# Cross-attention's mask and normalisation bias in the last row of the keys, in a transformer stack on one core

## The chip, the cores and the metric

The kernel runs on one core of a Trainium2 chip. The metric is the device time of one execution in microseconds (us). The core has TensorE (PE, matmuls; its weight loads are shown as PEld), VectorE (DVE), ScalarE (ACT), GpSimd (POOL) and SyncE (SP, which here issues the DMAs). Each engine works through its own instructions in the order in which they stand in the program, and waits for others by semaphores.

## What is computed

The reference is a stack of four blocks on x of 8 x 256 x 128, with a context of 8 x 64 x 64: a gated cross-attention (L0), a small cross-attention (L1), six decoder layers (L2) and a last attention with a softmax over the queries (L3). All is in float32. The change touches the second attention of each decoder layer. Cut to it:

```python
def _ln(x, g, b, eps=1e-05):
    m = jnp.mean(x, axis=-1, keepdims=True)
    v = jnp.mean(jnp.square(x - m), axis=-1, keepdims=True)
    return (x - m) / jnp.sqrt(v + eps) * g + b

def _mha(s, t, kv_w, q_w, o_w, o_b, mask):          # 16 heads of 64
    k, v = jnp.split(s @ kv_w, 2, axis=-1)
    q = t @ q_w
    ...
    scores = jnp.einsum('bhqd,bhkd->bhqk', q, k) * D ** (-0.5)
    scores = jnp.where(mask[:, None] == 0, jnp.float32(-1000000000.0), scores)
    attn = jax.nn.softmax(scores, axis=-1)
    o = jnp.einsum('bhqk,bhkd->bhqd', attn, v)
    ...
    return o @ o_w + o_b

def step(t, p):                                     # six times
    tn = _ln(t, norm_g, norm_b)
    t = _mha(tn, tn, skv, sq, sow, sob, tgt_mask) + t
    tn = _ln(t, norm_g, norm_b)
    t = _mha(src, tn, ckv, cq, cow, cob, src_mask) + t
    tn = _ln(t, pg, pb)
    t = t + (jax.nn.relu(tn @ w1 + b1) @ w2 + b2)
```

src is the context (64 keys for each batch entry), src_mask says which keys are hidden. norm_g and norm_b are one pair of vectors for all layers.

## The kernel before

The residual t stays in SBUF, two tiles of 128 rows for each of the 8 batch entries b.

**Order of the work.** Every stage registers small functions with at(tick, phase, function). At the end they are called in order of tick, then phase, and each engine's instructions are chained in just this order. So a tick is a round of the software pipeline, and the phase says where in the round a step stands in the queues of PE, DVE, ACT and POOL. In a layer, self-attention takes 4 ticks for each b (32 ticks), cross-attention 2 (16 ticks), the feed-forward 1 (8 ticks). T_ca is the first tick of a layer's cross-attention; b has its ticks T = T_ca + 2b and T + 1. Steps reach into the stages before and after.

**Folded weights.** Cross-attention's query and key weights are multiplied into one matrix AT for each head, and its value and output weights into WVO (plan_ca_weights). This is done at the end of self-attention: AT in tick T_ca - 4, WVO in T_ca - 3 (PE L1042, copies L1054 and L1052 on ACT). Then the keys of a head are AT times the context: they stand in the 128 dimensions of the normalised row, so that no query projection is left. keys_both makes the keys of two batch entries at once, in phase 3.7 of the ticks T_ca - 2, T_ca + 2, T_ca + 6, T_ca + 10: 16 matmuls into each of two PSUM tiles (L1079; the profile counts each float32 matmul of this form as two), and four copies to SBUF by ACT (L1085).

**Normalised rows.** ahead does them: statistics on DVE (L808, L809, phase 6 of tick T - 4, in the same tick as the keys for every second b), the scales on POOL (L814 to L821, phase 8.4), x minus mean times rstd on ACT (L827), a transpose on PE (L841), and, on the way out of PSUM, a multiplication by norm_g and an addition of norm_b on ACT (L843).

**A unit.** plan_weights_64 does a unit, 128 rows (one qt of a b), with 16 heads of 64 keys in a PSUM tile of two banks:

- scores, phase 1 of its tick: 16 matmuls in float32 (L341) and, after each four of them, four mask matmuls in bf16 (L348). A mask matmul has a stationary operand of zeros with ones in row 0, and a moving one, nm2, with 0 or -1e30 in row 0, so that it adds the mask to each row.
- lower, phase 2: ACT copies the scores to SBUF (e, L357), DVE takes each head's maximum (m, L359), POOL subtracts it (L360)
- exps, phase 8: exp on ACT (L366)
- divide, phase 2.4 of the next tick: sum and reciprocal on DVE (L370, L371), multiplication on POOL (L372)
- turn, phase 2.5 of the tick after: 32x32 transposes on DVE (L380)
- sums, phase 3.0 of the third tick after: 16 matmuls with the values (L388), and DVE adds the result to the residual (L1104)

The residual's bias is added by POOL (L290, phase 7), and the values are made by L303 (PE) and L309 (ACT).

**Self-attention beside it.** A tick there holds two units: scores L898, mask and minimum in one DVE operation (L912), exp on ACT (L917), the reciprocal L925 on DVE, the division L927 on POOL, transposes L937 on DVE, values L953 on PE with evictions L284 (DVE) and L286 (ACT), output projection L971 and its addition L978 on DVE (phase 8.2 of its tick).

**Buffers.** PSUM is a pool of four tiles of two banks, which all matmul results share. The SBUF tag "o" has four buffers, for self-attention's outputs, the folding and the feed-forward.

Of the kernel before, what the change touches and what calls it, by code (L numbers as in the profile page):

```python
# [8 lines left out]
F32 = mybir.dt.float32  # L9
I32 = mybir.dt.int32  # L10
BF16 = mybir.dt.bfloat16
AF = mybir.ActivationFunctionType
ALU = mybir.AluOpType
AX = mybir.AxisListType
PSUM = bass.MemoryType.PSUM

P = 128
B, S, D = 8, 256, 128
M, DM = 64, 64
NL, H, HD, FF = 6, 16, 64, 512  # L20
HC = H * HD // P
NT = B * S // P
QT = S // P
BIG = 1.0e30
# [3 lines left out]
def tile_xattn_stack(ctx: ExitStack, tc: tile.TileContext, io, out: bass.AP):  # L28
    nc = tc.nc

    const = ctx.enter_context(tc.tile_pool(name="const", bufs=1))
# [25 lines left out]
    def big(tag, bufs=4, shape=(P, 1024), dtype=F32):  # L57

        return heap.tile(list(shape), dtype, tag=tag, name=uniq(tag), bufs=bufs)
# [4 lines left out]
    def sm(shape, tag):  # L64
        return small.tile(shape, F32, tag=tag, name=uniq(tag))

    def load_const(name, shape):
        t_ = const.tile(shape, F32, tag=name, name=name)
        nc.sync.dma_start(out=t_, in_=io[name])
        return t_  # L70
# [7 lines left out]
    def column(name):  # L78
        v = io[name]
        t_ = const.tile([v.shape[0], 1], F32, tag=name, name=name)  # L80
        nc.sync.dma_start(out=t_, in_=v.unsqueeze(1))
        return t_
# [70 lines left out]

    norm_g = column("L2_norm_g")
    norm_b = column("L2_norm_b")
    pre_g = load_const("L2_pre_gT", [D, NL])
    pre_b = load_const("L2_pre_bT", [D, NL])
    ff_b1 = load_const("L2_ff_b1T", [P, NL, FF // P])
# [88 lines left out]
        return nm  # L247


    nm2 = const.tile([P, B, M], BF16, tag="nm2", name="nm2")  # L250
    nc.vector.memset(nm2, 0.0)
    ones0 = const.tile([P, 32], BF16, tag="ones0", name="ones0")
    nc.vector.memset(ones0, 0.0)
    nc.vector.memset(ones0[0:1], 1.0)


    def stats(xin, eps):
# [21 lines left out]
    def at(tick, phase, fn):  # L279
        plan.setdefault(tick, []).append((phase, fn))  # L280
# [30 lines left out]
        )  # L311
        return vw

    def plan_weights_64(tick, qt, qT, keys, values, mask, take):

        tl = {}

        def scores():  # L320
            sc = two_banks("sc").rearrange("p (q x) -> p q x", q=4)
            if mask is None:
                for i in range(4):
                    for a in range(4):
                        q = (i + 2 * (a // 2)) % 4
                        rows = slice(64 * (a // 2), 64 * (a // 2) + 64)
                        qb = 4 * qt + q
                        nc.tensor.matmul(
                            sc[32 * a : 32 * a + 32, q, :],
                            lhsT=qT()[rows, qb * 32 : (qb + 1) * 32],  # L330
                            rhs=keys()[rows, 4 * (a % 2) : 4 * (a % 2) + 4, :].rearrange(
                                "p h k -> p (h k)"
                            ),
                            start=True, stop=True,
                        )
                tl["sc"] = sc.rearrange("p q x -> p (q x)")
                return
            for q in range(4):
                qb = 4 * qt + q
                for a in range(4):  # L340
                    nc.tensor.matmul(  # L341
                        sc[32 * a : 32 * a + 32, q, :],
                        lhsT=qT()[:, qb * 32 : (qb + 1) * 32],
                        rhs=keys()[:, a].rearrange("p h k -> p (h k)"),
                        start=True, stop=False,
                    )
                for a in range(4):
                    nc.tensor.matmul(  # L348
                        sc[32 * a : 32 * a + 32, q, :], lhsT=ones0, rhs=mask,
                        start=False, stop=True,  # L350
                    )
            tl["sc"] = sc.rearrange("p q x -> p (q x)")

        def lower():
            sc = tl.pop("sc")
            e = big("e", shape=(P, 16, M))
            nc.scalar.copy(e.rearrange("p h k -> p (h k)"), sc)  # L357
            m = sm([P, 16], "m16")
            nc.vector.tensor_reduce(m, sc.rearrange("p (h k) -> p h k", k=M), AX.X, ALU.max)  # L359
            nc.gpsimd.tensor_tensor(  # L360
                e, e, m.unsqueeze(2).to_broadcast([P, 16, M]), ALU.subtract
            )
            tl["e"] = e

        def exps():
            nc.scalar.activation(tl["e"], tl["e"], AF.Exp)  # L366

        def divide():
            r = sm([P, 16], "r16")
            nc.vector.tensor_reduce(r, tl["e"], AX.X, ALU.add)  # L370
            nc.vector.reciprocal(r, r)  # L371
            nc.gpsimd.tensor_tensor(  # L372
                tl["e"], tl["e"], r.unsqueeze(2).to_broadcast([P, 16, M]), ALU.mult
            )

        def turn():
            e = tl.pop("e").rearrange("p (q h) (k x) -> p (h k) q x", q=4, x=32)
            eT = big("k", shape=(P, 8, 4, 32))
            for i in range(2):
                nc.vector.transpose(eT[:, 4 * i : 4 * i + 4], e[:, 4 * i : 4 * i + 4])  # L380
            tl["eT"] = eT

        def sums():
            ps = mm_tile()
            eT, vw = tl.pop("eT"), values()
            for s in range(8):
                g, r, k = s // 4, s // 2 % 2, s % 2
                nc.tensor.matmul(  # L388
                    ps[:, :D], lhsT=eT[:, s].rearrange("p q x -> p (q x)"),
                    rhs=vw[:, r, k, g, :], start=(s == 0), stop=(s == 7),  # L390
                )
            take(ps)

        at(tick, 1, scores)
        at(tick, 2, lower)
        at(tick, 8, exps)
        at(tick + 1, 2.4, divide)
        at(tick + 2, 2.5, turn)
        at(tick + 3, 3.0, sums)
# [212 lines left out]

    def mask_keys():
        mi = big("q", dtype=I32)
        mi = mi[0:1, : B * M].rearrange("p (b m) -> p b m", b=B)
        nc.sync.dma_start(out=mi, in_=io["mask_Bx1xS2_if1"].rearrange("b o m -> o b m"))
        nc.vector.tensor_scalar(nm2[0:1], mi, 0.0, -BIG, ALU.is_equal, ALU.mult)

    mask_bf = []

# [41 lines left out]
    def plan_l0(b, T):  # L662
        st = {}
# [67 lines left out]
        at(T + 2, 3.2, make_values)  # L731
        for qt in range(QT):
            plan_weights_64(
                T + qt, qt, lambda: st["q"], lambda: st["k"], lambda: st["VW"], None,
                lambda ps, qt=qt: add(qt, ps),
            )
        at(T + 4, 6, moments)
# [267 lines left out]
    def plan_ca_weights(l, T):  # L1005
# [54 lines left out]
            at(T - 4 + i, -0.5, lambda i=i: fetched(i))  # L1060
        at(T + 1, 8.05, regrouped)
        at(T + 2, 3.6, folded("AT", 0, lambda c: st[1][:, :, c, :], HD ** -0.5))
        at(T + 3, 3.6, folded("WVO", 1, lambda c: W["ca", l][2][:, c, :]))

    keys_of = {}

    def plan_ca(l, b, T):
        st = {}
        fold = W["fold", l]

        def keys_both():

            res = [big("q", shape=(D, 4, 4, M)) for _ in range(2)]
            for g in range(2):
                ps = two_banks("mm").rearrange("p (r a x) -> p r a x", r=2, a=4)
                for a in range(4):
                    for r in range(2):
                        rows = slice(r * DM, (r + 1) * DM)
                        nc.tensor.matmul(  # L1079
                            ps[:, r, a, :], lhsT=fold["AT"][rows, 4 * g + a, :],  # L1080
                            rhs=ctx2[rows, b : b + 2, :].rearrange("p b m -> p (b m)"),
                            start=True, stop=True,
                        )
                for i in range(2):
                    nc.scalar.copy(  # L1085
                        res[i][:, :, 2 * g : 2 * g + 2, :].rearrange("p a r k -> p r a k"),
                        ps[:, :, :, i * M : (i + 1) * M],
                    )
            keys_of[b], keys_of[b + 1] = res

        def make_values():
            st["VW"] = values_of(b, fold["WVO"])

        def res():
            st["tb"] = residual(b, W["ca", l][3])

        ahead(b, (T - 4, 6), (T - 3, 2.95), (T - 2, 2.9), norm_g, norm_b, st)
        if b % 2 == 0:
            at(T - 2, 3.7, keys_both)
        at(T + 2, 3.2, make_values)  # L1100
        at(T + 2, 7, res)

        def add(qt, ps):
            nc.vector.tensor_add(t[:, QT * b + qt, :], ps[:, :D], st["tb"][:, qt, :])  # L1104

        for qt in range(QT):
            plan_weights_64(
                T + qt, qt, lambda: st["tT"], lambda: keys_of[b], lambda: st["VW"],
                nm2[:, b].unsqueeze(1).to_broadcast([P, 4, M]), lambda ps, qt=qt: add(qt, ps),
            )  # L1110

    def plan_ff(l, b, T):
# [136 lines left out]
    last = {}  # L1249
# [68 lines left out]
```

## Time and profile before

| | us |
|---|---|
| median of three runs (2488.26 to 2490.18) | 2489.39 |
| the profiled execution | 2494.55 |
| its span, first to last instruction | 2492.8 |

The granted TensorE clock was 0.981 on average. In the first decoder layer the engines are busy as follows (us):

| stretch (us) | PE | DVE | ACT | POOL |
|---|---|---|---|---|
| 402 to 492, cross-attention of layer 0 (90) | 86.65 | 66.09 | 55.41 | 73.42 |
| 580 to 740, self-attention of layer 1 (160) | 160.00 | 137.12 | 126.14 | 86.09 |

The costliest groups are self-attention's (L917, L927, L912, L937, L953, L898). Of the lines named above, the page's list by groups has for cross-attention's parts (L0 uses the same helper for the unit, so counts of 112 hold 96 of cross-attention):

| line, engine | what | count | mean ns |
|---|---|---|---|
| L341 PE | scores, 128x256 f32 | 3072 | 382 |
| L357 ACT | copy of the scores | 112 | 999 |
| L359 DVE | maximum | 112 | 1224 |
| L360 POOL | subtraction | 112 | 1903 |
| L366 ACT | exp | 112 | 1063 |
| L370 DVE | sum | 112 | 1209 |
| L372 POOL | multiplication | 112 | 1902 |
| L380 DVE | transposes | 224 | 660 |
| L1085 ACT | copy of keys, 128x512 | 96 | 600 |
| L978 DVE | addition, 128x256, PSUM and SBUF | 48 | 388 |

A line of the profile's groups reads: line, engine, operation, tiles written and read, shapes, count, then busy time, mean time of one in ns, and the idle time of the engine before it with what ended it. In a timeline, the first number is the start in us from the span's start, the second the time that the merged instructions took, and a bracket at the end is the engine's idle time before it and who ended it. Matmuls overlap, so that the time of one is not its share of PE.

### The profile page before, as it was taken

How to read it: one execution, taken by the hardware profiler on the slowest of the kernel's cores; microseconds unless marked ns; L12 is line 12 of the kernel's file. 1: busy time of each engine (PE TensorE's matmuls, PEld its weight loads, DVE VectorE, ACT ScalarE, POOL GpSimd, SP SyncE). 2: the span in 40 equal slices, each digit the busy share in tenths (PEclk: the TensorE clock that was granted, in tenths of full speed). 3: DMA queues.
4: the chain of work that ended last, by engine and by line, in shares of the span. 5: the costliest groups of instructions: out<-in, count | busy, mean ns of one | idle time of the engine just before them, and what ended most of it. 6: DMA issues, size and time to landing. Idle time of an engine off the chain costs nothing.

```text
span 2492.8 us, 100152 instructions
## 1 busy us (share of the span) xinstructions
PE 2373.5 (95%) x42411; PEld 1749.2 (70%) x42411; DVE 1832.2 (74%) x5988; ACT 1725.5 (69%) x4528; POOL 1448.8 (58%) x2483
## 2 busy tenths in 40 slices
PE   8999999999999999999989999989999989999996
PEld 4667777676777676777776776776777777777774
DVE  4777887738887738888748888747888756888764
ACT  4577777667777657777657777657778657778651
POOL 3755556835556845556845555854556864555763
PEclk8999999999999999999999999999999999999997
DMA  6000022000022000022000012000012000010000
GB/s 174 2 4 18 20 77 56 2 12 20 20 70 63 2 12 20 20 62 67 6 7 24 20 54 71 11 3 20 20 55 78 12 3 20 20 42 23 2 1 18
DMA packets 102834, 76.89 MB, mean 31 GB/s; under 512 B 8113, under 2 KB 96881, under 8 KB 102386
## 3 DMA queue, kind: packets, MB, share of 16 engines
q1 hardware_dynamic: 101794, 70.16, 10.0%
q8 instruction: 334, 5.47, 0.9%
q14 instruction: 114, 0.93, 0.1%
q10 hardware_dynamic: 592, 0.33, 0.1%
HBM read 62.07 MB, written 8.39 MB: 28 GB/s over the span
## 4 chain that ended last, share of the span: by engine, by line
PE 69%; POOL 13%; DVE 8%; ACT 7%; issue 3%; POOLq 0%; DVEq 0%; ACTq 0%
PE mm L953 14%; PE mm L861 13%; PE sc L898 13%; PE mm L971 7%; PE mm L880 7%; POOL e L360 6%; PE mm L1120 3%; PE mm L1137 3%; DVE m L359 3%; POOL e L372 3%; ACT e L357 2%; PE mm L388 2%; ACT e L917 2%; DVE e L912 1%; PE sc L341 1%
## 5 line engine op out<-in xcount | busy, mean ns | idle before, releaser
L927 POOL TENSOR_SCALAR e<-e,rs 128x256 f32<-128x256 f32 x1536 | 702.5, 478 | 672.8 <-DVE rs L925 664.2
L917 ACT ACTIVATE e<-e,mn 128x256 f32<-128x256 f32 x1536 | 758.3, 495 | 145.7 <-DVE mn L912 141.5
L912 DVE CUSTOM_DVE_ANT_0 e<-sc,nm 128x256 f32<-128x256 f32 x1536 | 542.2, 418 | 98.7 <-PE sc L898 98.5
L937 DVE STREAM_TRANSPOSE eTc<-e 128x512 f32<-128x512 f32 x768 | 519.7, 697 | 69.1 <-POOL e L927 67.3
L953 PE MATMUL mm<-eTc,v 32*64 32x256 f32 x12288 | 377.6, 384 | 14.2 <-DVE eTc L937 7.0
L898 PE MATMUL sc<-k,q 64*32 64x256 f32 x12288 | 379.4, 380 | 6.2 <-DVE mn L912 4.2
L953 PEld LDWEIGHTS mm<-eTc,v 32*64 32x64 f32 x12288 | 283.2, 134 | 105.4 <-issue 25.0
L898 PEld LDWEIGHTS sc<-k,q 64*32 64x32 f32 x12288 | 220.7, 106 | 128.9 <-issue 48.9
L360 POOL TENSOR_TENSOR e<-e,m 128x1024 f32<-128x1024 f32 x112 | 213.1, 1903 | 132.1 <-DVE m L359 132.1
L917 ACT ACTIVATION_READ_ACCUMULATOR e<-e,mn 128x1 f32 x1536 | 287.2, 187 | 0.0
L359 DVE TENSOR_REDUCE m<-sc 128x16 f32<-128x1024 f32 x112 | 137.1, 1224 | 167.2 <-ACT e L357 167.2
L388 PE MATMUL mm<-v,k 128*128 128x128 f32 x1792 | 231.4, 284 | 5.4 <-DVE k L380 4.9
L388 PEld LDWEIGHTS mm<-v,k 128*128 128x128 f32 x1792 | 214.6, 196 | 26.9 <-issue 10.7
L341 PE MATMUL sc<-q,tT 128*32 128x256 f32 x3072 | 217.1, 382 | 0.0
L372 POOL TENSOR_TENSOR e<-e,r 128x1024 f32<-128x1024 f32 x112 | 213.0, 1902 | 0.7 <-DVE r L371 0.7
L366 ACT ACTIVATE e<-e 128x1024 f32<-128x1024 f32 x112 | 119.0, 1063 | 115.8 <-POOL e L360 115.8
L861 PE MATMUL mm<-tT,w_sk 128*128 128x256 f32 x768 | 189.6, 390 | 0.0
L971 PEld LDWEIGHTS mm<-w_sow,o 128*128 128x128 f32 x1536 | 175.1, 192 | 16.7 <-issue 14.4
L880 PE MATMUL mm<-w_sv,tT 128*32 128x256 f32 x3072 | 185.7, 382 | 0.0
L971 PE MATMUL mm<-w_sow,o 128*128 128x128 f32 x1536 | 183.4, 278 | 0.9 <-ACT WVO L1052 0.9
L286 ACT COPY v<-mm 128x1024 f32<-128x1024 f32 x96 | 97.1, 1012 | 120.7 <-PE mm L880 120.1
L861 PE MATMUL mm<-tT,w_sq 128*128 128x256 f32 x768 | 173.6, 379 | 0.0
(209 smaller groups left out, 3506.5 us busy)
## 6 DMA issues: line engine op xcount, KB each, us to landing
nm<-mask_d SPq DMA_DIRECT2D x192, 128.0 KB
wd<-o SPq DMA_DIRECT2D x48, 128.0 KB
w_sk<-in_L_sa_kv_dram SPq DMA_DIRECT2D x6, 512.0 KB
w_sv<-in_L_sa_kv_dram SPq DMA_DIRECT2D x24, 128.0 KB
w_sq<-in_L_sa_q_dram SPq DMA_DIRECT2D x6, 512.0 KB
w_sow<-in_L_sa_ow_dram SPq DMA_DIRECT2D x6, 512.0 KB
w_ckv<-in_L_ca_kv_dram SPq DMA_DIRECT2D x12, 256.0 KB
w_cq<-in_L_ca_q_dram SPq DMA_DIRECT2D x6, 512.0 KB
```

Source lines behind the costliest of these rows:

```text
L360: nc.gpsimd.tensor_tensor(e, e, m.unsqueeze(2).to_broadcast([P, 16, M]), ALU.subtract)
L372: nc.gpsimd.tensor_tensor(tl["e"], tl["e"], r.unsqueeze(2).to_broadcast([P, 16, M]), ALU.mult)
L388: nc.tensor.matmul(ps[:, :D], lhsT=eT[:, s].rearrange("p q x -> p (q x)"), rhs=vw[:, r, k, g, :], start=(s == 0), stop=(s == 7),)
L861: nc.tensor.matmul(ps[:, i * S : (i + 1) * S], lhsT=w[:, c * P : (c + 1) * P], rhs=st["tT"], start=True, stop=True,)
L880: nc.tensor.matmul(ps[32 * a : 32 * a + 32, i, :], lhsT=st["tT"][:, kb * 32 : (kb + 1) * 32], rhs=sv[:, a].rearrange("p g x -> p (g x)"), ...
L898: nc.tensor.matmul(sc[32 * a : 32 * a + 32, r, j, :], lhsT=st["q"][g][rows, a, qb * 32 : (qb + 1) * 32], rhs=st["k"][g][rows, a, :], start ...
L912: nc.vector.tensor_tensor_reduce(e[:, i, :], sc4[:, i, :], st["nm"][:, 2 * jj + i % 2, :], -1.0, 3.0 * BIG, ALU.add, ALU.min, mn[:, i : i ...
L917: nc.scalar.activation(e[:, i, :], e[:, i, :], AF.Exp, scale=-1.0, bias=mn[:, i : i + 1], accum_out=rs[:, i : i + 1],)
L927: nc.gpsimd.tensor_scalar(e[:, i, :], e[:, i, :], rs[:, i : i + 1], 1.0, ALU.mult, ALU.mult)
L937: nc.vector.transpose(eT[:, r, :, 2 * jj : 2 * jj + 2, :], e[:, 2 * r : 2 * r + 2, :].rearrange("p j (k x) -> p k j x", x=32),)
L953: nc.tensor.matmul(ops[a // 2][r * HD : (r + 1) * HD, a % 2, :S], lhsT=st["v"][kb // 4][rows, kb % 4, (2 * g + r) * HD : (2 * g + r + 1) * ...
L971: nc.tensor.matmul(st["ps"][:, j * D : (j + 1) * D], lhsT=st["oT"][c // 4][:, c % 4, j * P : (j + 1) * P], rhs=sow[:, c, :], start=(c == 0 ...
```

## The change

Rows of a normalised x have mean zero, so the sum over the 128 dimensions of x times a constant is zero: a number may be subtracted from all the entries of a key without a change of its scores. The changed kernel takes the last entry of the key from all of them (weigh, on the rows of AT, which it first multiplies by norm_g). The last dimension is then free. The row gets a constant 1 there (ahead is given last_off as scale and last_on as bias: 1 and 0 for all dimensions, 0 and 1 for the last), and the key gets there the sum of AT times norm_b, and the mask. The mask is added as the keys leave PSUM, from nm2, which now has 128 rows in float32 and is 0 but for its last row. The mask matmuls go, and with them their operand ones0. The copies of the keys by ACT become additions by DVE.

weigh stands in phase 2.9 of tick T_ca - 3 (T is T_ca - 6 in plan_ca_weights), between the fold of AT and that of WVO.

```diff
@@ tile_xattn_stack, constants
+    norm_rows = const.tile([P, 2, D], F32, tag="norm_rows", name="norm_rows")
+    for i, name in enumerate(("L2_norm_g", "L2_norm_b")):
+        nc.sync.dma_start(out=norm_rows[:, i, :], in_=io[name].partition_broadcast(P))
...
-    nm2 = const.tile([P, B, M], BF16, tag="nm2", name="nm2")
-    nc.vector.memset(nm2, 0.0)
-    ones0 = const.tile([P, 32], BF16, tag="ones0", name="ones0")
-    nc.vector.memset(ones0, 0.0)
-    nc.vector.memset(ones0[0:1], 1.0)
+    nm2 = const.tile([P, B, M], F32, tag="nm2", name="nm2")
+    last_on = ident[:, P - 1 : P]
+    last_off = const.tile([P, 1], F32, tag="last_off", name="last_off")
+    nc.vector.tensor_scalar(last_off, last_on, -1.0, 1.0, ALU.mult, ALU.add)
+    last_big = const.tile([P, 1], F32, tag="last_big", name="last_big")
+    nc.vector.tensor_scalar(last_big, last_on, -BIG, None, ALU.mult)
@@ plan_weights_64, scores
                         rhs=keys()[:, a].rearrange("p h k -> p (h k)"),
-                        start=True, stop=False,
-                    )
-                for a in range(4):
-                    nc.tensor.matmul(
-                        sc[32 * a : 32 * a + 32, q, :], lhsT=ones0, rhs=mask,
-                        start=False, stop=True,
+                        start=True, stop=True,
                     )
@@ mask_keys
-        mi = mi[0:1, : B * M].rearrange("p (b m) -> p b m", b=B)
-        nc.sync.dma_start(out=mi, in_=io["mask_Bx1xS2_if1"].rearrange("b o m -> o b m"))
-        nc.vector.tensor_scalar(nm2[0:1], mi, 0.0, -BIG, ALU.is_equal, ALU.mult)
+        mi = mi[:, : B * M].rearrange("p (b m) -> p b m", b=B)
+        nc.sync.dma_start(
+            out=mi, in_=io["mask_Bx1xS2_if1"].rearrange("b o m -> (b o) m").partition_broadcast(P)
+        )
+        nc.vector.tensor_scalar(nm2, mi, 0.0, last_big, ALU.is_equal, ALU.mult)
@@ plan_ca_weights
+        def weigh():
+
+            AT = st["AT"]
+            g, bias = (
+                norm_rows[:, i].unsqueeze(1).to_broadcast([P, HC, D]) for i in range(2)
+            )
+            z = big("o", shape=(P, HC, D))
+            nc.gpsimd.tensor_tensor(z, AT, bias, ALU.mult)
+            add = sm([P, HC], "add")
+            nc.vector.tensor_reduce(add, z, AX.X, ALU.add)
+            nc.gpsimd.tensor_tensor(AT, AT, g, ALU.mult)
+            last = sm([P, HC], "last")
+            nc.gpsimd.tensor_copy(last, AT[:, :, D - 1])
+            nc.gpsimd.tensor_tensor(
+                AT, AT, last.unsqueeze(2).to_broadcast([P, HC, D]), ALU.subtract
+            )
+            nc.gpsimd.tensor_copy(AT[:, :, D - 1], add)
+
+        at(T + 3, 2.9, weigh)
@@ plan_ca, keys_both
                 for i in range(2):
-                    nc.scalar.copy(
-                        res[i][:, :, 2 * g : 2 * g + 2, :].rearrange("p a r k -> p r a k"),
-                        ps[:, :, :, i * M : (i + 1) * M],
-                    )
+                    for r in range(2):
+                        nc.vector.tensor_tensor(
+                            res[i][:, :, 2 * g + r, :], ps[:, r, :, i * M : (i + 1) * M],
+                            nm2[:, b + i].unsqueeze(1).to_broadcast([P, 4, M]), ALU.add,
+                        )
@@ plan_ca
-        ahead(b, (T - 4, 6), (T - 3, 2.95), (T - 2, 2.9), norm_g, norm_b, st)
+        ahead(b, (T - 4, 6), (T - 3, 2.95), (T - 2, 2.9), last_off, last_on, st)
```

More of the change, by code (lines that the diff above doesn't have):

```diff
@@ L312, in values_of, with plan_weights_64 @@
         return vw
-    def plan_weights_64(tick, qt, qT, keys, values, mask, take):
+    def plan_weights_64(tick, qt, qT, keys, values, halves, take):
         tl = {}
@@ L321, in scores @@
             sc = two_banks("sc").rearrange("p (q x) -> p q x", q=4)
-            if mask is None:
+            if halves:
                 for i in range(4):
@@ L733, in plan_l0 @@
             plan_weights_64(
-                T + qt, qt, lambda: st["q"], lambda: st["k"], lambda: st["VW"], None,
+                T + qt, qt, lambda: st["q"], lambda: st["k"], lambda: st["VW"], True,
                 lambda ps, qt=qt: add(qt, ps),
@@ L1108, in plan_ca @@
                 T + qt, qt, lambda: st["tT"], lambda: keys_of[b], lambda: st["VW"],
-                nm2[:, b].unsqueeze(1).to_broadcast([P, 4, M]), lambda ps, qt=qt: add(qt, ps),
+                False, lambda ps, qt=qt: add(qt, ps),
             )
```

## The prediction

> **What bounds the kernel now.** I read the page first, then the busy time by stretch, the chain of waits inside one cross-attention stage, and last the timelines of DVE, POOL and ACT there. The page says PE:
>
> ```profile
> PE 2373.5 (95%) x42411; PEld 1749.2 (70%) x42411; DVE 1832.2 (74%) x5988; ACT 1725.5 (69%) x4528; POOL 1448.8 (58%) x2483
> PE 69%; POOL 13%; DVE 8%; ACT 7%; issue 3%; POOLq 0%; DVEq 0%; ACTq 0%
> L348 PE MATMUL sc<-nm,ones 128*32 128x256 bf16 x1536 | 112.3, 273 | 0.0
> ```
>
> L348 are the mask matmuls that go. Their 112.3 us is a union with matmuls running beside them, so it is no price. The PE timeline of one unit (a half batch entry, one tick) gives it:
>
> ```profile
> 421.03 0.64 PE L341 MATMUL sc<-q,tT 128*32 128x256 f32 x8
> 421.48 0.29 PE L348 MATMUL sc<-nm,ones 128*32 128x256 bf16 x4
> 421.59 0.61 PE L341 MATMUL sc<-q,tT 128*32 128x256 f32 x8
> ```
>
> From 421.48 to 421.59, four mask matmuls hold PE 0.11 us. There are four such groups in a unit (0.43 us) and 96 units: 41.5 us of PE. Whether that is time gained depends on the stage. The chain of waits in cross-attention (layer 0; start, duration, engine, tile, line):
>
> ```profile
> 442.34 1.90 POOL e L360
> 444.24 1.86 POOL e L372
> 446.10 0.69 POOL tb L290
> 446.79 0.08 issue
> 446.87 0.23 POOL ve L814
> ...
> 448.47 1.87 POOL e L360
> 450.39 0.94 issue
> 451.33 1.00 ACT e L357
> 452.35 1.24 DVE m L359
> 453.66 1.90 POOL e L360
> ```
>
> No PE in it. Two ticks take 11.32 us (442.34 to 453.66). In the first, 6.09 us, POOL has no gap: subtract, multiply, residual, scales, next subtract. The second, 5.23 us, is a loop: subtract 1.90, exp on ACT (the 0.94 "issue"), copy of the next scores 1.00, maximum on DVE 1.24, next subtract. Starts of L360 read from the trace: in all six layers the 15 gaps after the first are 5.23, 5.23, 8.42, 5.23, 6.09, 5.23, 6.09 and so on, alike within 0.01. Only the 8.42 has PE in it: the third unit, where PE still has the last output projection, values and keys to do. The stretch of four ticks (us, then PE, PEld, DVE, ACT, POOL busy):
>
> ```profile
> 441.52:463.90 22.38, 21.95 (x356) 16.13 (x356) 16.97 (x33) 14.34 (x20) 19.04 (x18) 1.00 0.01 2
> ```
>
> PE's 21.95 us fits inside the 22.63 us of two periods: it is nearly full but waits for the loop, so its relief there is not time. Where the new DVE work lands is the question:
>
> ```profile
> 444.75 0.25 DVE L1104 TENSOR_TENSOR t<-mm,tb 128x128 f32<-128x128 f32 x1
> 444.93 0.27 DVE L808 BATCH_NORM_STATS2 six<-t 128x6 f32<-128x128 f32 x1
> ...
> 445.63 0.18 DVE L809 BATCH_NORM_AGGREGATE mv<-six 128x2 f32<-128x6 f32 x1
> 446.96 1.23 DVE L359 TENSOR_REDUCE m<-sc 128x16 f32<-128x1024 f32 x1 [1.16 <-ACT e L357]
> ```
>
> In this tick (keys matmuls at 441.52) phase 3.7 lies between L1104 and L808. POOL's L814 reads mv, ready 445.81, and starts 446.87: 1.06 us of slack.
>
> [...] the copy L357 ends 452.33 and L359, which reads the same scores, starts 452.35. [...] with the scores ready, the copy at 451.33 still waits behind the exp of the unit before. So an add queued ahead of the statistics delays them. [...] in the window 490 to 500 us, with PE idle 2.6 us, the granted clock is 0.83. [...] L978, the same form, shows 0.39.
>
> **The change, part by part.**
>
> *Mask matmuls gone:* minus 0.43 us of PE a unit. In the loop worth nothing; in the third unit's tick two units' worth (0.87) is on PE's path.
>
> *Keys to DVE:* four ACT copies of 0.60 (2.05 us in sequence) become eight adds of 128x256 from PSUM on DVE. L978 starts its follower 0.31 us later, L912 (also PSUM, 256) 0.345; I take 0.32, so 2.6 us; both ends 2.5 and 2.8. In the ticks of pairs 3 and 4 (7th and 11th unit) mv comes at 445.81 + 2.6 = 448.41, L814 starts 0.1 later (as at 408.92 after 408.82), at 448.5 rather than 446.87: +1.64. The subtract behind it moves from 448.47 to 450.1; the maximum (448.5 to 449.7) is in time. The rest of the loop has no slack to take it back: +1.64 each, 3.3 a layer (bounds 1.5 and 1.8 each). ACT's relief brings the exp 0.4 us forward (444.64 to 444.27), off this path. PSUM: the two key tiles are held until about 448.2 instead of 444.8; PE, now 20.2 us of work in 24.3, can bear it.
>
> *weigh, once a layer, at T+3, 2.9* (tick T_ca-3): POOL, behind its first divide (ends 387.67), does three 128x1024 operations (1.90 each, as L372), two small copies (about 0.2 each), then the residual and the second divide: 388.35 becomes 394.4. DVE's reduction (1.21, as L370) is queued behind the reciprocal at 385.60 and ahead of the eviction at 385.66: it waits for z until 389.55 and ends 390.75. Then 0.57 eviction, reciprocal, transposes 1.25: the next scores pass on DVE starts 392.75 instead of 390.00, +2.75.
>
> *Keys of pair 1, tick T_ca-2:* the second transposes wait for POOL's late divide (396.3, end 397.0); then eight adds 2.6, statistics 0.9, transposes 1.3, L978: the scores pass comes at 402.3 instead of 397.82, +4.5. Through the last tick, where DVE had 0.97 us of idle to give back, the first cross maximum moves from 405.60 to 409.45: +3.9 (bounds: 1.5 if PE's waits there absorb more, 5 if the late eviction also holds back PE's PSUM tiles).
>
> *Third unit's tick:* PE restarts with the values at 407.59 + 4.0; the masks give back 0.87. Keys adds follow PE's two key groups, statistics, L978, maximum: subtract at 17.4 us after PE's restart, before 18.2. So 4.0 - 0.8 = about 3.3; rounded up 3.5 for the wait on the second key group. Bound above: PE waited here for L978 (0.17 us, all layers), which now stands behind the adds; if the scores keep that PSUM tile, +2.9 more.
>
> *The rest:* two broadcast loads at the start, a mask load that is wider (read at 153.2 us, issued at 121.7, so 30 us of cover), nm2 in f32, column constants: nothing; without cover, about 1 us once.
>
> Sum a layer: 3.5 + 3.3 = 6.8; six layers 40.8. After cross-attention comes the feed-forward, whose first ticks wait for POOL's scales too (PE idle 2.62 at 493.6), so nothing is taken back. The profiled run, 2494.55 (span 2492.8 and 1.75 around it), would become 2535.4; it stands 5.2 above the median, 2489.39, to which I add the same: **2530 us**.
>
> **Rivals.** (1) PE is what counts, and the adds hide in DVE's idle time (DVE is busy 16.97 of 22.38): the 41.5 us of masks are gained, less perhaps 1 us a layer for weigh: 2454. It decides where PE's own work is longer than the loop: after the change, if two ticks of the loop took less than PE's 10.1 us. For it: PE 95% busy. Against: the chain without PE, and POOL waiting for mv. (2) Only the loop's +3.3 a layer comes, weigh's block being absorbed by the self-attention tail, and the 0.8 is gained: 2.5 x 6 = 15: 2504. For it: DVE idles 1.58 and 0.71 us there. Against: the block is longer than all of it. (3) As forecast, and the scores wait for L978's tile: 9.7 a layer, 58: 2548. With half clock windows after PE's new gaps (1.7 us each), to 2558. (4) Gains and losses cancel: 2489; it needs weigh hidden and the adds under 0.14 us each, since 1.06 us is the slack for eight.
>
> **How the numbers follow.** Forecast (2515 to 2540) 0.50; (3) 0.22; (2) 0.14; (1) and what is faster otherwise 0.10; (4) 0.04. The range 2500 to 2556 leaves out (1), (4) and the top of (3), 0.17. What a measurement can tell from no change is about 0.2%, 5 us. Faster 0.10, same 0.04, slower 0.86.
>
> **What would show it.** In the changed trace: gaps between starts of the L360 subtract after the 7th and 11th unit 7.7 instead of 6.09, the others still 5.23 and 6.09; L814 released by DVE mv there; the eight adds 0.32 us apart just ahead of L808; DVE idle about 4 us before weigh's reduction, released by POOL z; the first cross subtract 4 us later against the last self-attention scores; the granted clock as before. The forecast is wrong if the cross stage gets shorter than 86.1 us (first to last subtract), which would mean PE held it; or if weigh's reduction waits for nothing.

## The result, and the profile after

The changed kernel took 2580.03 us (median of four, 2577.85 to 2583.40), the kernel before beside it 2489.78 us: a ratio of 1.0361, with a 95% interval of 1.0342 to 1.0380. It is slower by 90 us. The forecast had the side right and the size too small: 2530, with a range up to 2556.

The page of the changed kernel, PE and the others, and the shares of the chain that ended last:

```profile
PE 2400.6 (93%) x40875; PEld 1747.5 (68%) x40875; DVE 1900.2 (74%) x6185; ACT 1678.2 (65%) x4432; POOL 1490.3 (58%) x2513
PE 67%; DVE 12%; POOL 11%; ACT 5%; issue 3%; DMA 0%; SPq 0%; POOLq 0%; DVEq 0%; ACTq 0%
```

and, from the groups of instructions, the adds that are new on DVE:

```profile
L1108 DVE TENSOR_TENSOR q<-mm,nm 128x256 f32<-128x256 f32 x192 | 65.6, 411 | 15.4 <-PE mm L1101 15.4
```

PE has 1536 matmuls fewer and is busy 27 us longer: a sign of a slower clock (the mean granted clock went from 0.981 to 0.957, where the forecast said "as before"). DVE has gained the 65.6 us of the adds and is now 12% of the chain, where it was 8%.

A layer is cut here at four marks read from the traces: A, from its first self-attention scores pass on DVE to the first one in tick T_ca - 2; B, on to the first cross-attention subtract on POOL; C, to the last subtract; D, to the next layer's first scores pass. The table has means in us: of A without layer 0, of B and C over six layers, of D over its five. Half clock means that the trace records a granted TensorE clock of 0.5; the last column counts such stretches in the decoder layers (each 3.4 us or a multiple of it), with their total time:

| kernel | A | B | C | D | sum | half-clock stretches |
|---|---|---|---|---|---|---|
| before | 223.5 | 17.1 | 86.1 | 53.9 | 380.7 | 9, 41 us |
| after | 229.2 | 21.9 | 89.0 | 55.8 | 395.9 | 42, 164 us |

A layer lost 15.2 us: 10.4 at the end of self-attention (A and B), 2.9 in the cross stage, 1.8 behind it. Layer 0 lost less, since its A grew by 3.4 us (235.6 to 239.0) and not by 5.7. Six times 15.2, less this, is 89 us; the spans of the two profiled executions differ by 87.5 (2492.8 and 2580.3). So the loss is in the layers.

**The cross stage (C)** went as forecast. The chain of waits of the changed kernel through the tick of pair 3's keys:

```profile
451.90 0.18 DVE t L1127
452.07 2.65 DVE q L1108 x8
454.72 0.21 DVE six L811
...
455.35 0.20 DVE mv L812
455.54 0.08 issue
455.62 0.23 POOL ve L817
...
457.22 1.87 POOL e L361
...
460.08 1.00 ACT e L358
461.10 1.24 DVE m L360
...
462.41 1.90 POOL e L361
```

The adds are on the chain, and POOL's scales start when the statistics behind them are done. POOL's own timeline at that place:

```profile
453.13 0.73 POOL L296 TENSOR_TENSOR tb<-t,w_cob 128x256 f32<-128x256 f32 x1
455.62 0.22 POOL L817 TENSOR_SCALAR ve<-mv 128x2 f32<-128x2 f32 x1 [1.76 <-DVE mv L812]
```

POOL stood idle 1.76 us, which it did not before (0.08 "issue" at 446.79). The gap between subtracts, 6.09 before, is 7.77 (449.41 to 457.18); the next, 457.18 to 462.41, is 5.23 as before. The four ticks from 449.41:

```profile
449.41:473.73 24.32, 22.44 (x298) 15.52 (x296) 19.76 (x41) 12.45 (x17) 19.04 (x19) 0.93 0.01 2
```

DVE is busy 19.76 us where it had 16.97 in a stretch of 22.38, and four ticks take 24.32 instead of 22.63.

**The end of self-attention (A and B)** lost more than forecast. First PE in the kernel before, then DVE and PE in the changed kernel, all in layer 0, around the tick of weigh:

```profile
381.50 3.68 PE L953 MATMUL mm<-eTc,v 32*64 32x256 f32 x120 [0.38 <-ACT AT L1054]
...
387.62 1.25 PE L1042 MATMUL mm<-w_cow,o 64*64 64x128 f32 x18 [1.43 <-issue]
388.80 1.96 PE L898 MATMUL sc<-k,q 64*32 64x256 f32 x64
```


```profile
384.73 0.13 DVE L928 RECIPROCAL rs<-rs 128x4 f32<-128x4 f32 x1
389.14 1.22 DVE L1075 TENSOR_REDUCE add<-o 128x8 f32<-128x1024 f32 x1 [4.28 <-POOL o L1073]
390.28 0.68 DVE L290 COPY o<-mm 128x512 f32<-128x512 f32 x1
...
392.67 0.42 DVE L915 CUSTOM_DVE_ANT_0 e<-sc,nm 128x256 f32<-128x256 f32 x1 [0.44 <-PE sc L901]
```

```profile
391.01 3.31 PE L901 MATMUL sc<-k,q 64*32 64x256 f32 x64 [4.10 <-DVE o L290]
...
402.57 0.66 PE L956 MATMUL mm<-eTc,v 32*64 32x256 f32 x8 [0.15 <-PE sc L901]
404.85 5.37 PE L956 MATMUL mm<-eTc,v 32*64 32x256 f32 x120 [1.62 <-DVE t L981]
```

The pause at L1042 before the change is layer 0's alone; in layer 2 the same matmuls run through:

```profile
1149.89 1.96 PE L1042 MATMUL mm<-w_cow,o 64*64 64x128 f32 x32
1151.78 1.96 PE L898 MATMUL sc<-k,q 64*32 64x256 f32 x64
```

In the changed kernel DVE waits 4.28 us for POOL's z, as forecast. The eviction L290 behind it (L284 before the change) frees a PSUM tile late, so that PE stands 4.10 us, and then its scores take 3.31 us instead of 1.96, at a mean granted clock of 0.57. The same happens again at 404.85, behind L981, which stands behind pair 1's adds: 1.62 us of wait, and 5.37 us, at 0.68, for matmuls that took 3.68. Over the ten us around each of them the mean, in the column before the last two, is 0.83; in the kernel before it is 1.00 in both:

```profile
390.00:400.00 10.00, 8.98 (x124) 7.32 (x126) 6.88 (x25) 4.61 (x17) 8.15 (x13) 0.83 0.03 8
400.00:410.00 10.00, 8.23 (x202) 5.57 (x199) 8.83 (x36) 4.76 (x18) 4.27 (x11) 0.83 0.12 36
```

### The profile page after: what moved, and what is told of

It is laid out like the page before. It is cut to its first block, busy times and chain, and to the rows that moved or that the text cites. A ratio compares the mean times of both kernels' runs of the same rounds, so it can differ in the third digit from the quotient of the medians.

```text
span 2580.3 us, 97251 instructions
## 1 busy us (share of the span) xinstructions
PE 2400.6 (93%) x40875; PEld 1747.5 (68%) x40875; DVE 1900.2 (74%) x6185; ACT 1678.2 (65%) x4432; POOL 1490.3 (58%) x2513
## 4 chain that ended last, share of the span: by engine, by line
PE 67%; DVE 12%; POOL 11%; ACT 5%; issue 3%; DMA 0%; SPq 0%; POOLq 0%; DVEq 0%; ACTq 0%
PE mm L956 13%; PE mm L864 13%; PE sc L901 12%; PE mm L974 7%; PE mm L883 6%; POOL e L361 4%; PE mm L1143 3%; PE mm L389 3%; PE mm L1160 3%; DVE q L1108 3%; DVE m L360 2%; POOL e L373 2%; ACT e L358 2%; POOL e L930 2%; POOL rstd L819 1%
## 5 line engine op out<-in xcount | busy, mean ns | idle before, releaser
L956 PE MATMUL mm<-eTc,v 32*64 32x256 f32 x12288 | 398.4, 397 | 25.3 <-DVE t L981 9.7
L901 PE MATMUL sc<-k,q 64*32 64x256 f32 x12288 | 386.7, 386 | 34.1 <-DVE o L290 28.2
L956 PEld LDWEIGHTS mm<-eTc,v 32*64 32x64 f32 x12288 | 292.2, 138 | 129.4 <-issue 24.6
L389 PE MATMUL mm<-v,k 128*128 128x128 f32 x1792 | 251.2, 299 | 10.5 <-DVE k L381 10.5
L389 PEld LDWEIGHTS mm<-v,k 128*128 128x128 f32 x1792 | 231.9, 209 | 40.1 <-issue 16.3
L373 POOL TENSOR_TENSOR e<-e,r 128x1024 f32<-128x1024 f32 x112 | 213.0, 1902 | 0.7 <-DVE r L372 0.7
L347 PE MATMUL sc<-q,tT 128*32 128x256 f32 x3072 | 185.7, 382 | 0.0
```

The source lines that it names most:

```text
L373: nc.gpsimd.tensor_tensor(tl["e"], tl["e"], r.unsqueeze(2).to_broadcast([P, 16, M]), ALU.mult)
L389: nc.tensor.matmul(ps[:, :D], lhsT=eT[:, s].rearrange("p q x -> p (q x)"), rhs=vw[:, r, k, g, :], start=(s == 0), stop=(s == 7),)
L901: nc.tensor.matmul(sc[32 * a : 32 * a + 32, r, j, :], lhsT=st["q"][g][rows, a, qb * 32 : (qb + 1) * 32], rhs=st["k"][g][rows, a, :], start ...
L956: nc.tensor.matmul(ops[a // 2][r * HD : (r + 1) * HD, a % 2, :S], lhsT=st["v"][kb // 4][rows, kb % 4, (2 * g + r) * HD : (2 * g + r + 1) * ...
```

## The experiments

The ratios are to runs of the kernel before on the same chip, with their 95% intervals. The kernel before took 2489.78 to 2492.21 us (medians) in the four sets of runs. Theory A is the forecast's (engines waiting in line). Its rivals: B, the adds on DVE are what costs, not weigh; C, PE with less work loses its clock wherever it waits (its mean was 0.981 before the change and 0.957 after). The expectations count the half-clock stretches of the whole trace (15 before the change, 48 after), the tables those of the decoder layers.

| kernel | us | ratio | A | B | C | D | half-clock stretches |
|---|---|---|---|---|---|---|---|
| changed, reduction late | 2551.66 | 1.0250 (1.0228 to 1.0271) | 226.5 | 21.6 | 89.0 | 54.2 | 22 |
| changed, keys by ACT | 2528.48 | 1.0159 (1.0133 to 1.0185) | 229.3 | 17.4 | 85.7 | 55.3 | 22 |
| changed, no weigh | 2522.59 | 1.0133 (1.0112 to 1.0155) | 223.1 | 19.3 | 88.9 | 54.4 | 14 |
| before, no mask matmuls | 2497.38 | 1.0022 (1.0012 to 1.0032) | 224.0 | 16.8 | 85.7 | 55.1 | 16 |
| changed, mask matmuls kept | 2563.27 | 1.0287 (1.0271 to 1.0302) | 228.6 | 21.1 | 89.4 | 53.4 | 19 |
| changed, adds split | 2612.04 | 1.0484 (1.0466 to 1.0502) | 228.9 | 19.2 | 97.7 | 54.3 | 35 |
| changed, weigh early | 2522.85 | 1.0125 (1.0105 to 1.0146) | 223.5 | 19.3 | 89.1 | 54.9 | 20 |
| weigh early, adds split, exp later | 2561.41 | 1.0277 (1.0262 to 1.0292) | 223.8 | 18.5 | 96.1 | 54.3 | 30 |
| before, exp later | 2471.23 | 0.9918 (0.9902 to 0.9934) | 223.4 | 17.2 | 83.2 | 53.7 | 8 |
| before, exp later, no mask matmuls | 2455.60 | 0.9854 (0.9839 to 0.9869) | 223.8 | 16.8 | 80.3 | 54.3 | 11 |
| weigh early, adds behind, exp later | 2471.63 | 0.9917 (0.9900 to 0.9935) | 224.0 | 18.5 | 80.3 | 55.2 | 16 |
| weigh early, mask by PE in the keys, exp later | 2489.43 | 0.9990 (0.9981 to 0.9999) | 223.5 | 17.9 | 84.2 | 54.5 | 14 |

**The reduction late.**

```diff
-            add = sm([P, HC], "add")
-            nc.vector.tensor_reduce(add, z, AX.X, ALU.add)
+            st["z"] = z
...
-            nc.gpsimd.tensor_copy(AT[:, :, D - 1], add)
+        def weigh_last():
+            add = sm([P, HC], "add")
+            nc.vector.tensor_reduce(add, st.pop("z"), AX.X, ALU.add)
+            nc.gpsimd.tensor_copy(st["AT"][:, :, D - 1], add)
+        at(T + 3, 8.15, weigh_last)
```

> The changed kernel, with weigh's reduction on DVE and the copy behind it moved from phase 2.9 to phase 8.15 of the same tick, behind DVE's eviction and transposes; POOL's four operations stay. Theory A (the loss of about 9.7 us a layer at the end of self-attention comes from DVE waiting 4.3 us for POOL's z with PE's PSUM tiles behind it): the waits of PE for the eviction (4.1 to 4.8 us, once a layer) vanish, the half-clock windows there too, and the first cross subtract comes about 5.5 us a layer earlier: 2545 us (2530 to 2558). The two keys ticks in the loop stay at 7.77. Theory B (the adds of the keys on DVE are what delays that stage, weigh is covered): within 5 us of 2580. Theory C [...]: the half-clock windows stay at some 48 and the time near 2570.

28 us less than the changed kernel. DVE's wait for z fell from 4.3 to 1.6 us a layer, PE's wait for the eviction is gone, and another came in its place (PE's waits in this kernel; total, times, longest):

```profile
PE tp L844 <- ACT xn L830: 54.3, 42, 2.8
PE mm L1105 <- POOL AT L1085: 23.9, 6, 4.0
```

The keys now wait 4 us a layer for the last copy into AT. So theory A's wait is real, but moving one step moved the lateness: A and B fell by 3.0 us a layer, not by the 5.5 expected. The adds are not the whole, which speaks against B.

**The keys by ACT.** The eight adds become the four ACT copies of the kernel before, without the mask.

> The changed kernel with the keys copied by ACT as before; the addition of nm2 (the mask, which hides no key in these inputs) is left out. Theory A: the starts of the subtract in the loop go back to 6.09 from 7.77 after the 7th and 11th unit (3.4 us a layer), the third unit's gap falls below 7.9, and at the end of self-attention 2 to 4 us a layer go; weigh's wait stays: 2540 us (2525 to 2552). Theory B (adds are the whole): about 2490. Theory C: windows of half clock remain, 2560 or more.

The time is in the range of theory A. The gaps are back at 6.09, the third unit's at 8.01 (not below 7.9), B falls from 21.9 to 17.4. A stays at 229.3: its growth is weigh's alone.

**Without weigh.** Its at(...) line is left out.

> The changed kernel without weigh: norm_g, norm_b and the subtraction of the last entry are left out of the keys; adds on DVE stay. Theory A: no wait for z, the end of self-attention is late by 1.5 to 3 us a layer only (adds of pair 1), the cross stage stays 89.0 us long against 86.1: 2489 + 6 x 5 = 2519 (2508 to 2532). Theory B: above 2560. Theory C: many half-clock windows remain, 2540 or more.

A is as before, B is 2.1 us longer than before, C is 88.9. So of the loss of 10.4 us in A and B, the adds alone make 1.7 (this kernel against the one before the change), weigh alone 6.0 (the kernel with keys by ACT), and the two together 2.8 more. These parts include what the clock lost in each kernel.

**The kernel before without mask matmuls.**

```diff
-                        start=True, stop=False,
-                    )
-                for a in range(4):
-                    nc.tensor.matmul(
-                        sc[32 * a : 32 * a + 32, q, :], lhsT=ones0, rhs=mask,
-                        start=False, stop=True,
+                        start=True, stop=True,
                     )
```

> The kernel before without its mask matmuls and nothing else (the mask, which hides no key here, is left out). Theory A (the loop over POOL, ACT and DVE bounds cross-attention, not PE): only the third unit's 8.42 gets shorter, by some 0.9 us, the other gaps stay at 5.23 and 6.09: 2484 us (2478 to 2489). Rival, PE bounds it: 41 us less, 2448. Theory C: more half-clock windows than the 15 of before and slower than before.

This is the part of the change that was to gain, done alone: it gains nothing; it costs 0.2%, about the least that a measurement tells by the forecast's own words. The gaps stay at 5.23 and 6.09, and only the third unit's falls, 8.42 to 8.01. Its chain of waits has no PE in it:

```profile
451.64 1.90 POOL e L355
453.54 1.86 POOL e L367
...
457.77 1.87 POOL e L355
459.69 0.94 issue
460.63 1.00 ACT e L352
461.65 1.24 DVE m L354
462.96 1.90 POOL e L355
```

That the time rose and did not fall by 5 us was not what theory A expected; it is what C expected. D is longer by 1.2 us, with more half clock. C, the stage, gained 0.4 us a layer.

**The mask matmuls kept in the changed kernel,** with an operand of zeros, to give PE its work back:

```diff
+                for a in range(4):
+                    nc.tensor.matmul(
+                        sc[32 * a : 32 * a + 32, q, :], lhsT=ones0,
+                        rhs=zeros2.unsqueeze(1).to_broadcast([P, 4, M]),
+                        start=False, stop=True,
+                    )
```

> The changed kernel with the mask matmuls still issued, with an operand of zeros (they add nothing), so that PE has its old amount of work in cross-attention. Theory A (waits of the engines set the time): third unit's gap back from 7.9 towards 8.4, nothing else: 2580 to 2585 us. Theory C (fewer matmuls let the clock fall): fewer than 40 half-clock windows against 48, the stretch from the last cross subtract to the next self-attention falls from 55.8 to about 54 us, 2565 to 2575 us.

Theory A failed here and C's signs came: with matmuls that compute nothing the kernel is 17 us faster, a little more than C expected. D falls by 2.4 us, A and B by 1.4, though the stage C rises by 0.4. The windows of ten us behind the cross stage, in the changed kernel and then in this one:

```profile
496.00:506.00 10.00, 7.20 (x91) 5.20 (x91) 9.17 (x20) 5.63 (x9) 9.41 (x13) 0.91 0.01 2
506.00:516.00 10.00, 8.02 (x71) 6.74 (x71) 5.00 (x12) 4.78 (x10) 7.89 (x13) 0.84 0.03 8
516.00:526.00 10.00, 9.70 (x62) 8.64 (x62) 1.75 (x7) 3.94 (x10) 2.02 (x5) 0.91 0.00 0
```

```profile
496.00:506.00 10.00, 7.33 (x102) 5.75 (x87) 8.77 (x21) 6.44 (x10) 9.50 (x12) 1.00 0.01 2
506.00:516.00 10.00, 8.02 (x78) 6.56 (x77) 4.88 (x12) 5.09 (x13) 7.09 (x13) 1.00 0.03 8
516.00:526.00 10.00, 9.38 (x64) 8.21 (x63) 3.34 (x15) 5.04 (x13) 3.37 (x10) 1.00 0.00 0
```

PE is busy for much the same time in both, but at 0.91, 0.84 and 0.91 in the first. The traces tell what went ahead of such a fall. Each holds a record of the granted clock, and in all fourteen the changes in it lie on a grid of 3.413 us; in the changed kernel the two falls shown above are half clock from 391.5 to 394.9 us and from 405.1 to 408.5, one window each. The windows of the decoder layers that have the full clock, cut by that grid and sorted by PE's idle time in them, as the profile shows it, and how many of them are followed by half clock:

| PE idle in the window | before | after | all fourteen traces |
|---|---|---|---|
| under 1.0 us | 0 of 629 | 0 of 593 | 0 of 8688 |
| 1.0 to 2.0 us | 6 of 21 | 29 of 35 | 143 of 360 |
| 2.0 us or more | 3 of 3 | 13 of 13 | 135 of 137 |

So in these traces PE's idle time in one such window goes with the fall, and it was often far less than the window: the one ahead of 405.1 us, with the wait of 1.62 us in it, has 1.77 us.

This also fixes D. It took 52.7 to 52.8 us in the 11 cases without half clock in it, 54.2 to 54.7 in the 36 with one window of it, 55.3 to 55.8 in the 23 with nearly two or two. The changed kernel has 2.8 us of PE idle time in the window just ahead of or across D's start in each layer, and another with 1.8 some 7 us into D; a layer lasts 116.0 windows, so that each falls alike. With the mask matmuls kept, the idle time around D's start lies across two windows in three layers of five, with 1.8 us at most in one, and no half clock follows. How much of the 17 us is shorter idle time, and how much is where the windows happened to fall, is not told apart.

**The adds split,** four behind the statistics, four in the next tick:

```diff
+            at(T - 2, 3.7, keys_both)
+            at(T - 2, 6.5, lambda: keys_out(0))
+            at(*((T - 1, 6.5) if b else (T - 2, 6.5)), lambda: keys_out(1))
```

> The changed kernel with the adds of the keys behind the statistics (phase 6.5 instead of 3.7), four in the keys tick and four in the next tick (for pair 1 all eight in the keys tick). Theory A (the adds cost because POOL's scales and the next maximum stand behind all eight): gaps after the 7th and 11th unit back to 6.09 to 6.2 with as many adds as before, cross stage 86 us, weigh's wait unchanged: 2580 - 20 = 2560 us (2552 to 2568). Rival (DVE's added busy time costs wherever it stands): the stage stays 89 us, 2580.

A miss, and a telling one. The gaps after the 7th and 11th unit did go back to 6.09 to 6.2, but the next ones, and the one after the third unit's, went from 5.23 to between 7.7 and 9.5. PE's timeline there:

```profile
455.24 2.05 PE L389 MATMUL mm<-v,k 128*128 128x128 f32 x16
461.19 3.64 PE L347 MATMUL sc<-q,tT 128*32 128x256 f32 x32 [3.91 <-DVE q L1114]
```

The second key tile is held in PSUM into the next tick, and the scores that are to use that tile wait 3.91 us for its adds; then their 32 matmuls take 3.64 us, against 1.93 for those of the unit at 469.05. A step that is cheap for DVE was dear through the buffer that it held.

**weigh early.** The same steps on the turned query weights, which are ready some ticks before the fold; the reduction stands a tick behind the operation that it needs.

```diff
-        at(T + 3, 2.9, weigh)
+        at(T - 2, 8.5, weigh_bias)
+        at(T - 1, 8.15, weigh_sum)
+        at(T - 1, 8.5, weigh_gain)
+        at(T, 8.5, weigh_last)
```

> The changed kernel with weigh's work done on the turned query weights some ticks ahead of the fold (the same sum, since the fold is linear), each DVE step a tick behind the POOL step that it needs; all else as changed. Theory A (weigh costs by its place, not by its work): the end of self-attention as in the kernel without weigh, 19.3 us from its last scores to the first cross subtract, 2523 us (2517 to 2532). Rival (weigh's busy time on POOL costs anywhere): 2540 or more.

As without weigh, 2522.85 against 2522.59: weigh's work is free here, its place was not.

**The three together, adds split.**

```diff
-        at(tick, 8, exps)
+        at(tick + 1, 2.05, exps)
```

> Weigh early, the adds split behind the statistics, and the exp of a unit moved behind the copy of the next unit's scores (phase 2.05 of the next tick instead of 8 of its own). Theory A (cross-attention is a loop POOL subtract, ACT exp, ACT copy, DVE maximum): the loop is open, POOL's 9.84 us or PE's 10.1 us for two ticks set the pace instead of 11.32: cross stage 78 to 82 us instead of 86.1, 2465 us (2445 to 2490), faster than the kernel before. Rival (the stage has another bound at the same pace): gaps stay at 5.23 and 6.09, 2500.

A miss, by the key tile again: PE waits 69.8 us in total for L1129, the adds. Some gaps are 3.57 and 3.72, though, which they could not be while the exp stood in the loop of 5.23.

**The kernel before with the exp later,** the same one line:

> The kernel before, with the exp of a unit moved behind the copy of the next unit's scores (phase 2.05 of the next tick instead of 8 of its own). Theory A (the chain subtract, exp, copy, maximum is what paces cross-attention, PE close behind it): the loop is open, PE's 22.0 us for four ticks take the place of 22.63, a layer gains 2 to 4 us: 2475 us (2465 to 2487). Rival (POOL or the exp's later end holds the pace): 2489 or slower.

20 us faster than before, with no more than the order of two ACT instructions, and C makes 2.9 us a layer of it: the loop was the bound. **And without the mask matmuls too:**

> The kernel before with the exp moved in the same way and without its mask matmuls (the mask, which hides no key here, is left out). Theory A: now that PE sets the pace, the mask matmuls' 0.43 us a unit count: 5 to 6.5 us a layer less than with the masks and the exp moved, 2442 us (2430 to 2455). Rival (PE's work never counts): no difference to the same kernel with masks.

Now they count: 15.6 us, 2.9 us a layer in C, where they had been worth 0.4. It is less than the 5 to 6.5 expected. Seven of the fifteen gaps fall by 0.41 to 0.44 us, the masks of one unit; the other eight, with POOL's 6.09 among them, stay.

**weigh early, all eight adds behind the statistics in the keys tick, the exp later:**

> The changed kernel with weigh early, the exp moved, and all eight adds behind the statistics in the keys tick, so that no PSUM tile of keys is held into the next tick. Theory A: no wait of PE for the adds of about 4 us as with the split ones; the keys tick costs some 1.3 us and the others are PE's or POOL's pace (about 10.2 for two ticks): cross stage 80 to 84 us, 2485 us (2465 to 2505). Rival (DVE, with 20.1 us for four ticks, becomes the bound together with PE's tiles): stage 88 or more, 2520.

C is 80.3 us, to a tenth that of the kernel without any mask and any adds. DVE at the keys tick:

```profile
456.18 0.26 DVE L811 BATCH_NORM_STATS2 six<-t 128x6 f32<-128x128 f32 x1
456.48 0.18 DVE L812 BATCH_NORM_AGGREGATE mv<-six 128x2 f32<-128x6 f32 x1
456.58 2.71 DVE L1129 TENSOR_TENSOR q<-mm,nm 128x256 f32<-128x256 f32 x8
459.37 1.22 DVE L360 TENSOR_REDUCE m<-sc 128x16 f32<-128x1024 f32 x1
```

The same eight adds in the same 2.71 us; they end as the copy of the next scores ends (458.32 + 1.01), and cost nothing in C. This kernel is faster than the one before (0.9900 to 0.9935) and than the changed one, and equal to the one before with the exp moved: what C gains without the mask matmuls (2.9) goes back in A and B (1.9, most of it in B, where pair 1's adds still stand in self-attention) and D (1.6, more half clock). All eight adds behind the statistics with the exp in its old place were not run, so the two parts are not told apart here.

**The mask by PE in the keys,** two bf16 matmuls of 512 columns into each key tile, keys copied by ACT, with weigh early and the exp later:

> Weigh early, the exp moved, and the mask put in the last row of the keys by PE itself: two bf16 matmuls of 512 columns into each key tile, with a stationary operand that has a 1 for the last row; the keys are copied by ACT as before the change. Theory A: DVE is as before, PE gives 1.73 us and takes 0.85 for four ticks: cross stage 79 to 82 us, 2462 us (2448 to 2478), faster than the kernel before. Rival: as in the kernel before, 2489 or more.

A miss: the keys tick's gap is 8.33 us, against 7.06 with the adds and also without any mask. PE's path has the 1.27 us: from the first matmul into the key tiles to the scores behind the keys it takes 3.25 us (458.43 to 461.68), and 1.98 with the adds (454.34 to 456.32). The expected 0.85 is 0.11 us for 256 columns, as in the forecast, times eight; two of these matmuls took 0.53 us from start to start, and the keys behind them (eight matmuls into a tile, which the profile counts as 16) 1.10 instead of 0.99. C is 84.2. It is not better than the adds.

## Why the prediction was right and wrong

- **That cross-attention is a loop over POOL, ACT and DVE, and that the masks' 41.5 us of PE are not time: right.** The masks' removal alone gave a ratio of 1.0022; the exp's move alone 0.9918. The row of gaps does not go on to its end as the forecast says: the last four are 5.23, 5.23, 5.40 and 6.08 before, and nearly the same after, which bears on nothing here.
- **+1.64 in each of two keys ticks: right.** 7.77 - 6.09 = 1.68, by the named wait of L814 (now L817) for mv.
- **The third unit's tick, minus 0.8: in sign, but smaller.** 8.42 became 7.89, minus 0.5; the scores did not wait for L978's tile, so this part of rival (3) did not come.
- **weigh "+2.75" and pair 1 "+4.5", then "+3.9" at the first cross maximum: the step that failed.** It is the term for the end of self-attention, in a layer 10.4 us (A and B) instead of 3.9. The mechanism was the named one (DVE waits for z: 4.28 us measured, 3.9 by the forecast's own times), but the term was mis-sized. Four things made it larger:
  - POOL's first two operations took 2.34 and 2.35 us, not 1.90.
  - The hold of PE's PSUM tiles stood only in the bound ("5 if the late eviction also holds back PE's PSUM tiles"), and it was the case: PE stood 28.2 us in all for L290 and 9.7 for L981.
  - PE's clock fell after both stands, to a mean of 0.57 and 0.68 over the matmuls behind them: 3.31 - 1.96 and 5.37 - 3.68 make 3.0 us in layer 0. The forecast had the half clock as an addition to rival (3) alone, 10 us in all, when the window of ten us that it quotes already showed 0.83 with 2.6 us of idle PE, 1.7 us of clock.
  - The forecast was read from layer 0, which is not like the others. There PE paused 1.43 us at L1042 even before the change, and DVE idled 1.58 us, which the "+2.75" uses up. From the first scores pass in tick T_ca - 4 to the one in T_ca - 2, layer 0 went from 15.08 to 18.62 us, 3.5 more, but layer 2 from 13.42 to 18.53, 5.1 more.

  How the missing 6.5 us divide among the four was not measured.
- **"nothing is taken back" behind the stage: right, but a cost was left out.** D grew by 1.8 us a layer, and this is the clock's: in all kernels D follows the half clock in it (52.7, 54.2 to 54.7 or 55.3 to 55.8 us), whatever else was changed. The forecast expected the granted clock as before.
- **The range** added bounds term by term, with the PE tiles and the clock as separate small cases, while here they followed from the same wait: a wait of DVE held a tile, the tile stopped PE, and half clock came behind the stop. 10.4 - 3.9 in A and B and 1.8 in D are 8.3 of the 8.4 us that a layer lost beyond the 6.8 forecast.

## What to carry to other kernels

An engine that is 95% busy can still be waiting for a loop of others: read the chain of waits inside the stage before paying with other engines for its relief, and open the loop first (here one line, the exp behind the next copy, made the mask matmuls count). When a step is put into a queue, look at what stands behind it, at the buffer that it holds until it runs, and at who needs that buffer; the same eight adds cost the cross stage 1.68 us ahead of the statistics, up to 4.2 when half of them kept a PSUM tile a tick longer, and nothing behind the statistics with the loop open. Put steps on weights where their inputs are ready and nobody waits: the work of weigh was free a few ticks earlier. And read a forecast's times from more than one layer: the first one had a pause, and so a slack, that the others lacked.

## What the runs showed of the hardware

- In the fourteen traces the granted clock changed on a grid of 3.413 us. In the decoder layers half clock followed no full-clock window with less than 1.0 us of PE idle time, 143 of 360 with 1.0 to 2.0, and 135 of 137 with 2.0 or more.
- Fewer matmuls came with more half clock. Without its mask matmuls the kernel before went from 9 to 16 stretches in the decoder layers; the changed one has 42 without them and 19 with zero ones put back, and is then 17 us faster.
- On POOL, a 128x1024 product with an operand repeated over the outer dimension (a row of 128 for each of eight heads) took 2.34 us (L1073), with one repeated over the inner dimension 1.90 us (L373; the subtraction in weigh, of this kind and of the same shape, also took 1.90).
